# Sorting one 48-place block for two pairs of graphs at a time, and the last 16 places for four

## The chip, the cores and the metric

The kernel runs on one core of one Trainium2 chip. The metric is device time in microseconds (us), the median of three executions. A separate, profiled execution gives the page and the trace that this document reads. Its own time differs a little from the median, so shares and sums are made against the profiled execution.

## The reference

Sixteen graphs of 1,024 nodes with 64 channels pass through two layers. The first layer is the costly one. For each graph it takes a 0/1 adjacency, drops some edges of nodes with more than ten neighbours, and then, for each node and each channel by itself, sorts the values of the remaining neighbours and reads three quantiles:

```
nd = adj_d > 0
vals = jnp.where(nd[..., None], x[:, None, :, :], jnp.inf)
s = jnp.sort(vals, axis=2)
nv = nd.sum(2)
for tau, w in zip(TAUS, WTS):          # 0.25, 0.5, 0.75
    pos = tau * (nv - 1)               # v_lo, v_hi: s at floor(pos), ceil(pos)
    agg = agg + w * (v_lo + frac * (v_hi - v_lo))
h = relu((x + agg) @ W1 + b1);  y = (h @ W2 + b2) * mask
```

The second layer is three graph convolutions (adjacency times features times weights, with normalisation) and one product over their concatenation. Both layers start with a layer norm and end with a residual sum.

## The kernel before

**Pairs and places.** Graphs are worked in eight pairs (0 to 7): the 128 partitions are 2 graphs of 64 channels. For each graph, `prepare` ranks the nodes by their number of neighbours; the rank is the node's *place*. Places are cut into blocks of like degree, each with a number of slots that holds the neighbours of every node in it (`BLOCKS`, lines 39 and 40, as first place, end, fewest neighbours, slots):

```
BLOCKS = ((0, 200, 1, 11), (200, 392, 10, 13), (392, 592, 12, 15), (592, 768, 14, 17),
          (768, 888, 16, 19), (888, 960, 17, 21), (960, 1008, 19, 26))
TAIL = (1008, 1024, 21, 42)
```

Blocks are called 0 to 6 here; block 6 has 48 places, the tail 16.

**Gather and sort.** `gather` (line 959) brings the neighbours' values into slots: VectorE compares slot numbers (line 987) to make a one-hot tile `s`, TensorE multiplies it with the features `hp` into PSUM (line 1018), ScalarE copies the result to `g` (line 1023). `quantiles` (line 925) then runs a fixed comparator network of VectorE min and max instructions on `g` and a spare tile `t` (line 935; each instruction covers up to a two-dimensional grid of slots, times the width in places). ScalarE makes the coefficients from `z` (lines 868 and 871), and VectorE multiplies (941) and sums (950). The networks are tables in `NETS`, one for each number of slots: one row is one instruction. The number of elements that an instruction covers is its slots times the number of places sorted together.

**Order.** The program is emitted by generators. `weave` (line 1106) runs the sort of block n, and between its instructions takes steps of other generators by share of the sort's work: the gather of block n+1, and steps of `prepare` for the next pair (93 steps, split by `SHARES`; lines 31 and 1447). In the last sort (block 6), the next pair's block 0 is gathered. In pair 7, which has no next pair, seven steps of `later` (the rest of layer one, and layer two) stand beside each sort instead, and what is left of `later` follows the last sort. The framework's planner then orders each engine's instructions by the order of emission, by what is ready in its own model, and by which buffers are free. So an instruction can stand ahead of its place in the code.

**Preparation.** `prepare_one` loads the adjacency in eight rows of tiles `a`. ScalarE takes its sign (671), VectorE checks it for values other than 0 and 1 (673, into a throw-away tile `junk_v`), TensorE transposes (678). VectorE clears the diagonal by a multiplication with `other_h` (686). Then come the edge dropping (711 to 755), eight ScalarE passes that count larger keys (770, into `junk`), and GpSimd row writes of the edges to memory by place (`live_d`, 778). `find_live` loads them back by GpSimd (`lp`, 794, two buffers), transposes (809), counts, and `number_slots` (838) numbers the slots. The second half of the numbering falls into the next pair's first steps.

**Tails.** The tail of each of pairs 0 to 6 is gathered during the sort of block 5 of its own pair, stored (`tail_d`, line 1069), and sorted with others: pairs 0 to 3 in pair 4, pairs 4 to 6 in pair 7 (`TAILS`, line 43; `sort_tails`, line 1090). Pair 7's own tail is sorted alone at the end (line 1476, n = 7).

**Buffers.** `g` has two buffers, `t`, `z`, `coef` and `agg` one, `hp` two, `s` two, PSUM `pg` three.

## Time and profile before

| what | us |
| --- | --- |
| median of 3 executions | 3143.26 (3135.98 to 3146.2) |
| profiled execution, its own time | 3163.56 |
| its span, first to last instruction | 3161.8 |
| VectorE (DVE) busy | 2559.8 |
| TensorE (PE) busy | 2599.2 |
| ScalarE (ACT) busy | 1696.2 |
| GpSimd (POOL) busy | 619.5 |
| first sort instruction of pair 0, from the start | 230.3 |
| last sort instruction, from the start | 2832.2 |
| granted TensorE clock, mean | 0.915 of full |

The names in the page and the trace are PE for matmuls, PEld for weight loads, DVE for VectorE, ACT for ScalarE, POOL for GpSimd and SP for the queue of loads and stores. L935 is line 935 of the kernel before. A group's line has the tiles written and read, partitions by elements, the count, and after the bar the busy time. A stretch's line has its bounds and length, then each engine's busy time with its instructions, the granted clock, the share of the DMA engines and GB/s. A line of the timeline has the start, the time to the end of the last of its instructions, the engine and line, and in brackets the idle time before it and what ended it.

### The profile page before, as it was taken

The page shows a single profiled execution, that of the slowest core. Times are in us where ns is not written, and L with a number is a line of the kernel's source. Part 1 is how long each engine was busy: PE and PEld are TensorE (multiplying, and loading weights), DVE is VectorE, ACT ScalarE, POOL GpSimd, SP SyncE. Part 2 cuts the span into 40 slices and gives each one's busy share as a digit, 9 for nine tenths or more (in the row PEclk, how much of TensorE's full clock was granted, in tenths as well). Part 3 has the DMA queues.
Part 4 walks back from the last instruction along what each step waited for, and adds up shares of the span by engine and source line. Part 5 has one row for each costly group of instructions (what it writes and reads, how often), then busy time and mean ns, then how long its engine had stood idle before and what let it go on. Part 6 is the DMA issues. An engine that isn't in the chain of part 4 may idle for free.

```text
span 3161.8 us, 67201 instructions
## 1 busy us (share of the span) xinstructions
PE 2599.2 (82%) x27849; PEld 1697.4 (54%) x27849; DVE 2559.8 (81%) x5895; ACT 1696.2 (54%) x3292; POOL 619.5 (20%) x545
## 2 busy tenths in 40 slices
PE   2678978898888889885798889888986688977778
PEld 1445655565556556653565566456643456644445
DVE  4149889998999799989998999899976979963332
ACT  4764666567557755774367557745853223332221
POOL 5110161022102200330022103300422530311110
PEclk9779999999899999997899999999987799988989
DMA  4131022111211212122111211211113011122211
GB/s 138 46 104 60 3 67 70 56 55 52 66 57 54 64 56 68 46 72 47 42 64 51 66 56 57 67 56 63 48 36 75 9 41 26 49 55 54 54 54 42
DMA packets 221082, 177.45 MB, mean 56 GB/s; under 512 B 189024, under 2 KB 189152, under 8 KB 216672
## 3 DMA queue, kind: packets, MB, share of 16 engines
q1 hardware_dynamic: 141824, 125.88, 13.1%
q0 software_dynamic: 17408, 37.81, 3.9%
q10 hardware_dynamic: 61536, 9.39, 1.7%
q8 instruction: 219, 3.59, 0.5%
q14 instruction: 95, 0.78, 0.1%
HBM read 124.44 MB, written 48.55 MB: 55 GB/s over the span
## 4 chain that ended last, share of the span: by engine, by line
DVE 40%; PE 29%; ACT 12%; DMA 8%; issue 6%; another core or an unknown queue 2%; POOL 2%; ACTq 1%; DVEq 0%; POOLq 0%; SPq 0%
PE pg L1018 11%; DVE t L935 10%; DVE s L987 9%; DVE g L935 8%; PE pg L1200 5%; ACT junk L770 3%; DMA a<-in_adj 3%; DMA lp<-live_d 3%; DVE junk_v L673 2%; PE pr L845 2%; DVE g_tails L935 1%; DVE t_tails L935 1%; PE keys L763 1%; PE pf L1216 1%
## 5 line engine op out<-in xcount | busy, mean ns | idle before, releaser
L1018 PE MATMUL pg<-s,hp 128*64 128x400 bf16 (+11 forms) x16848 | 1366.5, 313 | 172.3 <-DVE s L987 138.1
L1018 PEld LDWEIGHTS <-hp 128*64 128x64 bf16 x16848 | 894.5, 112 | 553.9 <-issue 109.6
L987 DVE TENSOR_SCALAR s<-r 128x3200 bf16<-128x3200 bf16 (+25 forms) x1312 | 623.6, 521 | 103.6 <-PE pg L1018 74.9
L778 POOL DMA_INDIRECT live_d<-edge,place x128 | 261.1, 2040 | 1354.3 <-DVE place L773 1149.9
L1023 ACT COPY g<-pg 128x400 f32<-128x400 f32 (+10 forms) x384 | 169.0, 443 | 399.4 <-PE pg L1018 363.1
L935 DVE TENSOR_TENSOR t<-g 128x600 f32<-128x600 f32 (+9 forms) x524 | 315.5, 626 | 34.0 <-ACT g L1023 33.2
L1200 PE MATMUL pg<-adjT,xw 128*64 128x512 fp8e4 x2304 | 284.5, 398 | 52.8 <-ACT xw L1185 25.7
L935 DVE TENSOR_TENSOR g<-t 128x96 f32<-128x96 f32 (+16 forms) x555 | 283.2, 537 | 1.2
L1243 POOL DMA_INDIRECT agg<-agg_d,place x128 | 171.2, 1338 | 495.2 <-PE pt L1131 258.2
L671 ACT ACTIVATE edge<-a 128x1024 fp8e4<-128x1024 f32 x128 | 135.1, 1058 | 214.4 <-DMA a<-in_adj 213.9
L1200 PEld LDWEIGHTS <-xw 128*64 128x64 bf16 x2304 | 140.1, 114 | 182.4 <-issue 42.0
L868 ACT ACTIVATE coef<-z,bias 128x200 f32<-128x200 bf16 (+6 forms) x480 | 173.9, 405 | 102.3 <-DVE agg L950 66.0
L935 DVE TENSOR_TENSOR t<-t 128x192 f32<-128x192 f32 (+20 forms) x447 | 207.8, 475 | 0.2
L871 ACT ACTIVATE coef<-coef,wcol 128x200 f32<-128x200 f32 (+7 forms) x512 | 189.6, 403 | 9.3 <-issue 7.1
L673 DVE SCALAR_TENSOR_TENSOR junk_v<-a 128x1024 fp8e4<-128x1024 f32 x128 | 155.4, 1214 | 24.4 <-DMA a<-in_adj 24.4
L845 PE MATMUL pr<-liveT,upto 128*128 128x512 fp8e4 (+2 forms) x384 | 127.4, 350 | 53.1 <-ACT r L851 46.9
L770 ACT ACTIVATE junk<-keys,minus 128x1024 fp8e4<-128x1024 f32 x128 | 144.3, 1128 | 38.1 <-PE keys L763 34.3
L851 ACT CAST r<-pr 128x592 bf16<-128x592 f32 (+1 forms) x256 | 142.5, 585 | 41.1 <-PE pr L847 32.1
L794 POOL DMA_DIRECT2D lp<-live_d x128 | 89.4, 699 | 376.9 <-PE pt L809 319.3
L812 ACT ACTIVATE liveT<-pt 128x1024 fp8e4<-128x1024 f32 x128 | 130.3, 1034 | 50.5 <-PE pt L809 47.1
L752 ACT ACTIVATE edge<-q,bias 128x1024 fp8e4<-128x1024 f32 x128 | 141.8, 1108 | 22.6 <-PE q L747 22.6
L725 ACT ACTIVATE stays<-cs,back 128x1024 f16<-128x1024 f32 x128 | 136.7, 1111 | 31.1 <-PE cs L721 15.9
(182 smaller groups left out, 3879.4 us busy)
## 6 DMA issues: line engine op xcount, KB each, us to landing
a<-in_adj SPq DMA_DIRECT2D x128, 512.0 KB
adjT_d<-edgeT SPq DMA_DIRECT2D x16, 1024.0 KB
lp<-live_d POOLq DMA_DIRECT2D x128, 128.0 KB
adjT<-adjT_d SPq DMA_DIRECT2D x16, 1024.0 KB
room<-in_x SPq DMA_DIRECT2D x16, 256.0 KB
h_d<-room SPq DMA_DIRECT2D x16, 256.0 KB
h_again<-h_d SPq DMA_DIRECT2D x16, 256.0 KB
xt<-in_x SPq DMA_DIRECT2D x16, 256.0 KB
```

Of the source, the lines that this page charges most:

```text
L673: nc.vector.scalar_tensor_tensor(junk, a, 1.0, a, ALU.is_equal, ALU.not_equal, accum_out=odd[:, b, t : t + 1], saturate=False)
L770: nc.scalar.activation(junk, keys, AF.Sign, bias=minus[:, t : t + 1], accum_out=above[:, t : t + 1], saturate=False)
L778: sent = nc.gpsimd.indirect_dma_start(out=live_d[b][:, :], out_offset=bass.IndirectOffsetOnAxis(ap=place[:, b, t : t + 1], axis=0), in_=ed ...
L845: nc.tensor.matmul(out=pr[:, o], lhsT=upto, rhs=liveT[:, u, sl], start=True, stop=(u == 0))
L868: nc.scalar.activation(coef[:, i, :], z[:, at], AF.Abs, bias=bias(rank - (slots + 1) // 2 + tau), scale=sign)
L871: nc.scalar.activation(coef[:, i, :], coef[:, i, :], AF.Relu, bias=wcol[:, q : q + 1], scale=-w)
L935: nc.vector.tensor_tensor(view(bufs, o, n1, n2), view(bufs, a, n1, n2), view(bufs, b, n1, n2), ALU.max if op else ALU.min)
L987: nc.vector.tensor_scalar(s[:, k, :, us, w0:], r[:, :, us, at + w0 : at + W], float(LIVE + 1 + k0 + k), None, ALU.is_equal)
L1018: summed = nc.tensor.matmul(out=pg[x * C : (x + 1) * C, ks, w0:], lhsT=st.hp[:, part, x, u, :], rhs=s[:, ks, x, u, w0:], start=(whole and ...
L1023: nc.scalar.copy(g[:, k0 : k0 + n, :], pg)
L1200: nc.tensor.matmul(out=pg[cs, :], lhsT=part[:, u, cs], rhs=adjT[x][:, u, sl], start=(u == 0 and k == 0), stop=(u == NT - 1 and k == len(xw ...
L1243: nc.gpsimd.indirect_dma_start(out=agg[:, t, x, :], out_offset=None, in_=agg_d[b][:, :], in_offset=bass.IndirectOffsetOnAxis(ap=place[:, b ...
```

## The change

Block 6 (`MID`) is no longer sorted in each pair. An even pair gathers it during the sort of block 4, into the front of the buffer that block 5's gather fills next, and stores it in memory (`part_d`). The odd pair after it loads those rows into one half of a double-width tile, gathers its own block 6 into the other half, and sorts 96 places together (`rows_of_pairs`, `sort_pairs`). Even pairs so have six sorts, odd ones seven, and `SHARES` gets one row for each kind. In even pairs the next pair's block 0 and the tail are gathered during the sort of block 5.

The tails of pairs 4 to 7 are sorted together: pair 7's tail is gathered during its block 0, straight into the joint tile. Seven steps of `later` now stand beside that joint sort, and the separate last sort is gone.

Four networks are replaced. Instructions and comparator outputs (slots written) of each, before and after:

| slots | instructions | outputs | product instructions after it |
| --- | --- | --- | --- |
| 13 | 29, 29 | 85, 85 | 1, 1 |
| 15 | 31, 30 | 106, 106 | 1, 1 |
| 19 | 60, 57 | 158, 158 | 1, 2 |
| 26 | 95, 85 | 249, 249 | 1, 2 |

The network of 13 needs 15 spare slots instead of 17. The tail's (187 instructions, 550 outputs, 3 products) stays.

The diagonal is cleared by a bitwise and on 32-bit words. The two throw-away tiles share the two buffers of `lp`. In `later`, `h` lies in the buffer of the former `hp`. Aggregates of pairs 6 and 7 are complete only after the last joint sort (`done.sent`).

The diff, with the networks' rows and repeated edits left out:

```diff
-SHARES = (10, 9, 17, 24, 20, 13, 0)
+SHARES = ((12, 12, 21, 27, 21, 0), (10, 9, 17, 24, 20, 13, 0))
...
 
-TAILS = {4: (0, 4), 7: (4, 7)}
+TAILS = {4: (0, 4), 7: (4, 8)}
 TAIL = (1008, 1024, 21, 42)
+
...
-    13: (17, {3: 2, 4: 5, 5: 1, 6: 4, 7: 7, 8: 0, 9: 3, 10: 6}, (
...
+    13: (15, {3: 1007, 4: 1010, 5: 1006, 6: 1011, 7: 1009, 8: 1005, 9: 1012, 10: 1008}, (
...
-    15: (17, {3: 1001, 4: 1006, 5: 1003, 7: 1002, 8: 1000, 10: 1005, 11: 1004}, (
...
+    15: (17, {3: 7, 4: 4, 5: 9, 7: 8, 8: 6, 10: 5, 11: 10}, (
...
-    19: (24, {4: 8, 5: 5, 6: 6, 9: 4, 10: 9, 13: 10, 14: 7}, (
...
+    19: (24, {4: 1003, 5: 1016, 6: 1006, 9: 1012, 10: 1004, 13: 1014, 14: 1005}, (
...
-    26: (40, {6: 7, 7: 12, 8: 10, 9: 14, 12: 8, 13: 13, 17: 9, 18: 11, 19: 15}, (
...
+    26: (40, {6: 1000, 7: 1007, 8: 1002, 9: 1005, 12: 1003, 13: 1004, 17: 8, 18: 1001, 19: 1006}, (
...
+
+    off_diag = const.tile([P, P // 4], I32, name="off_diag")
+    nc.vector.tensor_scalar(off_diag[:, :].bitcast(U8), ident, -255.0, 255.0, ALU.mult, ALU.add)
...
-    TW = TAIL[1] - TAIL[0]
-    tail_d = [dram.tile([P, TAIL[3], TW], F32, name=f"tail_d{p}") for p in range(NP)]
-
-    tail_z = const.tile([P, len(TAUS), NP, TW], BF16, name="tail_z")
+    MW, TW = (b[1] - b[0] for b in (BLOCKS[MID], TAIL))
+    part_d = {
+        MID: [dram.tile([P, BLOCKS[MID][3], MW], F32, name=f"mid_d{p}") for p in range(NP)],
+        MID + 1: [dram.tile([P, TAIL[3], TW], F32, name=f"tail_d{p}") for p in range(NP)],
+    }
+
+    part_z = {
+        MID: const.tile([P, len(TAUS), 2, MW], BF16, name="mid_z"),
+        MID + 1: const.tile([P, len(TAUS), 4, TW], BF16, name="tail_z"),
+    }
...
     def diagonal(e):
 
+        e = e[:, :, :].bitcast(I32)
         dims = [list(d) for d in e.ap]
-        return bass.AP(tensor=e.tensor, offset=e.offset, ap=[dims[0], [N + P, NT], [1, P]])
+        return bass.AP(tensor=e.tensor, offset=e.offset, ap=[dims[0], [(N + P) // 4, NT], [1, P // 4]])
 
...
             nc.scalar.activation(edge[:, t, :], a, AF.Sign, saturate=False)
-            junk = work.tile([P, N], F8, tag="junk_v", name="junk_v")
+            junk = work.tile([P, N // 4], I32, tag="lp", bufs=2, name="junk_v")[:, :].bitcast(F8)
...
         own = diagonal(edgeT)
-        nc.vector.tensor_tensor(own, own, other_h[:, None, :].to_broadcast([P, NT, P]), ALU.mult, saturate=False)
+        nc.vector.tensor_tensor(own, own, off_diag[:, None, :].to_broadcast([P, NT, P // 4]), ALU.bitwise_and)
...
         for t in range(NT):
-            junk = work.tile([P, N], F8, tag="junk", name="junk")
+            junk = work.tile([P, N // 4], I32, tag="lp", bufs=2, name="junk")[:, :].bitcast(F8)
             nc.scalar.activation(
...
 
-    def gather_block(st, n, pools, home=None):
+    def gather_block(st, n, pools, home=None, into=None, first=-0.2, end=0.9):
+
 
         work, ps, rows = pools
         block = (BLOCKS + (TAIL,))[n]
@@ -1060,20 +1066,24 @@
         pool, tag, bufs = home or (rows, "g", 2)
 
         def groups():
-            if n == 0:
+            if n >= MID:
+                z = part_z[n]
                 for q in range(len(TAUS)):
-                    nc.gpsimd.tensor_copy(tail_z[:, q, st.p, :], st.z[:, q, TAIL[0] : TAIL[1]])
-            st.g[n] = pool.tile([P, slots, j1 - j0], F32, tag=tag, bufs=bufs, name="g")
-            send(pools, (yield from gather(st, block, st.g[n], pools)))
-            if n == len(BLOCKS) and st.p < NP - 1:
-                nc.scalar.dma_start(out=tail_d[st.p][:, :, :], in_=st.g[n])
-
-        return Steps(groups()), -(-slots // per_group(block)), -0.2, 0.9
+                    nc.gpsimd.tensor_copy(z[:, q, st.p % z.shape[2], :], st.z[:, q, j0:j1])
+            to = into
+            if to is None:
+                to = st.g[n] = pool.tile([P, slots, j1 - j0], F32, tag=tag, bufs=bufs, name="g")
+            send(pools, (yield from gather(st, block, to, pools)))
+            in_place = st.p % 2 if n == MID else st.p == NP - 1
+            if n >= MID and not in_place:
+                nc.scalar.dma_start(out=part_d[n][st.p][:, :, :], in_=to)
+
+        return Steps(groups()), -(-slots // per_group(block)), first, end
 
     def sort_block(st, n, pools):
 
         work, ps, rows = pools
-        block = (BLOCKS + (TAIL,))[n]
+        block = BLOCKS[n]
         j0, j1, _, slots = block
         if n == 0:
 
@@ -1082,26 +1092,32 @@
             st.done = 0
         t = rows.tile([P, plan(block)[3], j1 - j0], F32, tag="t", bufs=1, name="t")
         yield from quantiles(work, block, (st.g[n], t), st.z[:, :, j0:j1], st.agg[:, j0:j1])
-        while st.done + P <= j1 or (j1 >= TAIL[0] and st.done < j1):
+        while st.done + P <= j1 or (n == MID - 1 and st.done < j1):
             cols = slice(st.done, min(st.done + P, j1))
             waiting.append((st.p, st.agg, cols, st.done))
             st.done = cols.stop
 
-    def sort_tails(first, end, pools):
+    def rows_of_pairs(n, first, end, sent, pools):
 
         work, ps, rows = pools
-        W = (end - first) * TW
-        g = rows.tile([P, TAIL[3], W], F32, tag="g", bufs=2, name="g_tails")
+        block = (BLOCKS + (TAIL,))[n]
+        W = block[1] - block[0]
+        g = rows.tile([P, block[3], (end - first) * W], F32, tag="g", bufs=2, name="g_pairs")
+        for p in range(first, sent):
+            nc.scalar.dma_start(out=g[:, :, (p - first) * W : (p - first + 1) * W], in_=part_d[n][p][:, :, :])
+        return g
+
+    def sort_pairs(n, first, end, g, pools):
+
+        work, ps, rows = pools
+        block = (BLOCKS + (TAIL,))[n]
+        W = block[1] - block[0]
+        whole = (end - first) * W
+        t = rows.tile([P, plan(block)[3], whole], F32, tag="t", bufs=1, name="t_pairs")
+        agg = work.tile([P, whole], F32, tag="agg_pairs", name="agg_pairs")
+        yield from quantiles(work, block, (g, t), part_z[n].rearrange("p q p2 w -> p q (p2 w)"), agg)
         for p in range(first, end):
-            nc.scalar.dma_start(out=g[:, :, (p - first) * TW : (p - first + 1) * TW], in_=tail_d[p][:, :, :])
-        yield 0.0
-        t = rows.tile([P, plan(TAIL)[3], W], F32, tag="t", bufs=1, name="t_tails")
-        agg = work.tile([P, W], F32, tag="agg_tails", name="agg_tails")
-        yield from quantiles(
-            work, TAIL, (g, t), tail_z[:, :, first:end].rearrange("p q p2 w -> p q (p2 w)"), agg
-        )
-        for p in range(first, end):
-            waiting.append((p, agg, slice((p - first) * TW, (p - first + 1) * TW), TAIL[0]))
+            waiting.append((p, agg, slice((p - first) * W, (p - first + 1) * W), block[0]))
 
     def weave(sort, *others):
 
...
             nc.sync.dma_start(out=rows_of(graphs[x]), in_=res[:, :, x, :])
         yield
 
-    def later(pools, done):
+    def later(pools, keep, done):
 
         one, ps = pools
+
+        old_hp = keep.tile([P, 3, 2, NT, C], BF16, tag="hp", bufs=2, name="old_hp")
 
         def first(p):
             assert p < done.sent
             xt = one.tile([P, NT, 2, C], F32, tag="xt", bufs=2, name="xt")
-            h, agg = (one.tile([P, NT, 2, C], F32, tag=k, name=k) for k in ("h", "agg"))
+            h = old_hp.rearrange("p a x t c -> p (a x t c)")[:, : 2 * N * 2 * C // P].bitcast(F32)
+            h = h.rearrange("p (t x c) -> p t x c", x=2, c=C)
+            agg = one.tile([P, NT, 2, C], F32, tag="agg", name="agg")
             mk = one.tile([P, NT, 2], U8, tag="mk", name="mk")
             mask = one.tile([P, NT, 2], F32, tag="mask", name="mask")
...
@@ -1443,25 +1462,39 @@
                     return (yield from prepare(p + 1, early))
 
                 ahead = Steps(coming(st, p))
-                for n in range(last):
-                    steps = (ahead, SHARES[n], 0.0, 1.0)
+
+                paired = p % 2
+                for n in range(MID + paired):
+                    steps = (ahead, SHARES[paired][n], 0.0, 1.0)
+                    sort = sort_block(st, n, pools) if n < MID else sort_pairs(MID, p - 1, p + 1, both, pools)
                     if n == 0 and p in TAILS:
 
-                        tails = sort_tails(*TAILS[p], pools)
-                        next(tails)
-                        weave(sort_block(st, n, pools), steps)
-                        weave(tails, gather_block(st, n + 1, pools))
-                    elif n == last - 1:
+                        tails = rows_of_pairs(MID + 1, *TAILS[p], TAILS[p][1], pools)
+                        weave(sort, steps)
+                        weave(sort_pairs(MID + 1, *TAILS[p], tails, pools), gather_block(st, n + 1, pools))
+                    elif n == MID - 1 + paired:
                         ahead.rest()
                         to_come = ahead.result
-                        weave(sort_block(st, n, pools), gather_block(to_come, 0, pools))
-                    elif n == last - 2:
+                        tail = () if paired else (gather_block(st, MID + 1, pools, (early[0], "a", 2)),)
+                        weave(sort, *tail, gather_block(to_come, 0, pools))
+                    elif n == MID - 1:
+                        both = rows_of_pairs(MID, p - 1, p + 1, p, pools)
                         weave(
-                            sort_block(st, n, pools), gather_block(st, n + 1, pools),
-                            gather_block(st, last, pools, (early[0], "a", 2)), steps,
+                            sort, gather_block(st, MID, pools, into=both[:, :, MW:]),
+                            gather_block(st, MID + 1, pools, (early[0], "a", 2)), steps,
+                        )
+                    elif n == MID - 2 and not paired:
+
+                        j0, j1, _, slots = BLOCKS[n + 1]
+                        room = st.g[n + 1] = pools[2].tile([P, slots, j1 - j0], F32, tag="g", bufs=2, name="g")
+                        size = BLOCKS[MID][3] * MW
+                        mid = room.rearrange("p s w -> p (s w)")[:, :size].rearrange("p (s w) -> p s w", w=MW)
+                        weave(
+                            sort, gather_block(st, MID, pools, into=mid, end=0.35),
+                            gather_block(st, n + 1, pools, into=room, first=0.4), steps,
                         )
                     else:
-                        weave(sort_block(st, n, pools), gather_block(st, n + 1, pools), steps)
+                        weave(sort, gather_block(st, n + 1, pools), steps)
                 st = to_come
             for _ in st.number:
                 pass
@@ -1472,20 +1505,23 @@
             late = (one, inner.enter_context(tc.tile_pool(name="ps_late", bufs=2, space=PSUM)))
             done = Pair()
             done.sent = TAILS[NP - 1][0]
-            ahead = Steps(later(late, done))
-            for n in range(last + 1):
+            ahead = Steps(later(late, keep, done))
+            for n in range(MID):
                 steps = (ahead, STEPS, 0.0, 1.0)
+                sort = sort_block(st, n, pools)
                 if n == 0:
-                    tails = sort_tails(*TAILS[NP - 1], pools)
-                    next(tails)
-                    weave(sort_block(st, n, pools), steps)
-                    weave(tails, gather_block(st, n + 1, pools))
+                    tails = rows_of_pairs(MID + 1, *TAILS[NP - 1], NP - 1, pools)
+                    weave(sort, gather_block(st, MID + 1, pools, into=tails[:, :, -TW:]), steps)
+                    weave(sort_pairs(MID + 1, *TAILS[NP - 1], tails, pools), gather_block(st, n + 1, pools), steps)
                     continue
-                if n < last:
-                    weave(sort_block(st, n, pools), gather_block(st, n + 1, pools), steps)
+                if n < MID - 1:
+                    weave(sort, gather_block(st, n + 1, pools), steps)
                 else:
-                    weave(sort_block(st, n, pools), steps)
-                done.sent = NP - 1
+                    both = rows_of_pairs(MID, NP - 2, NP, NP - 1, pools)
+                    weave(sort, gather_block(st, MID, pools, into=both[:, :, MW:]), steps)
+
+                done.sent = NP - 2
+            weave(sort_pairs(MID, NP - 2, NP, both, pools), (ahead, STEPS, 0.0, 1.0))
             send(pools)
             done.sent = NP
             ahead.rest()
```

## The prediction

> **What bounds the kernel now.** I read the page first (engine shares, the forty slices, the chain), then cut the span into stretches, then looked at single instructions inside them. From the page, the busy times, the slices and the chain's shares by engine:
>
> ```profile
> PE 2599.2 (82%) x27849; PEld 1697.4 (54%) x27849; DVE 2559.8 (81%) x5895; ACT 1696.2 (54%) x3292; POOL 619.5 (20%) x545
> ...
> PE   2678978898888889885798889888986688977778
> DVE  4149889998999799989998999899976979963332
> ...
> DVE 40%; PE 29%; ACT 12%; DMA 8%; issue 6%; another core or an unknown queue 2%; POOL 2%; ACTq 1%; DVEq 0%; POOLq 0%; SPq 0%
> ```
>
> VectorE is at nine tenths from slice 3 to slice 35 and TensorE close behind; only the first three slices and the last four (the second half of the network, 330 us) are not VectorE's. Averages hide which of the two ends last, so I took the starts of each block's first sort instruction as cuts. A "stretch" is the time from one block's first sort instruction to the next one's. The seven stretches (blocks 0 to 6) of pair 5, columns length, then busy PE, PEld, DVE, ACT, POOL with their instructions, clock, DMA:
>
> ```profile
> 1789.90:1825.30 35.40, 32.70 (x397) 21.75 (x393) 34.58 (x48) 19.93 (x42) 0.00 (x0) 0.95 0.15 48
> 1825.30:1865.30 40.00, 33.48 (x429) 23.11 (x427) 40.00 (x58) 17.91 (x35) 0.00 (x0) 1.00 0.23 82
> 1865.30:1914.00 48.70, 45.68 (x563) 31.60 (x560) 48.70 (x81) 29.94 (x50) 0.00 (x0) 1.00 0.14 45
> 1914.00:1960.20 46.20, 40.85 (x486) 29.16 (x486) 44.92 (x88) 34.28 (x63) 23.36 (x10) 0.93 0.15 51
> 1960.20:2003.50 43.30, 38.75 (x449) 25.87 (x447) 40.20 (x122) 35.08 (x66) 13.60 (x13) 0.98 0.19 53
> 2003.50:2041.10 37.60, 34.08 (x392) 19.64 (x392) 29.59 (x102) 29.77 (x66) 9.68 (x11) 0.98 0.23 67
> 2041.10:2083.80 42.70, 34.70 (x345) 19.52 (x346) 42.12 (x127) 24.18 (x54) 8.67 (x3) 0.88 0.25 77
> ```
>
> Six of seven are VectorE's to within 3 us. Only stretch 5 (block of 72 places) leaves it idle, 8 us: there the preparation of the next pair binds. The sum is 293.9 us, DVE 280.1, PE 260.2. So VectorE work taken out of a stretch should come off the time, until PE or the preparation binds.
>
> In pair 7 (no next pair; steps of the second half are woven in), the tails' sort, block 6 and the lone tail of 16 places:
>
> ```profile
> 2440.30:2491.60 51.30, 19.17 (x187) 14.24 (x185) 51.30 (x209) 13.23 (x46) 37.64 (x15) 0.68 0.09 21
> ...
> 2747.00:2782.80 35.80, 32.94 (x293) 21.04 (x294) 34.84 (x136) 13.90 (x34) 3.38 (x4) 0.95 0.11 19
> 2782.80:2832.20 49.40, 36.20 (x258) 21.76 (x254) 33.06 (x210) 15.71 (x49) 12.36 (x13) 0.83 0.27 75
> ```
>
> **What an instruction costs.** The timeline of VectorE inside the lone tail:
>
> ```profile
> 2807.43 0.17 DVE L935 TENSOR_TENSOR t<-g,t 128x16 f32<-128x16 f32 x1
> 2807.51 0.21 DVE L935 TENSOR_TENSOR g<-g 128x64 f32<-128x64 f32 x1
> 2807.65 0.16 DVE L935 TENSOR_TENSOR g<-g,t 128x16 f32<-128x16 f32 x1
> 2807.73 0.18 DVE L935 TENSOR_TENSOR g<-t 128x32 f32<-128x32 f32 x1
> ```
>
> Durations overlap: 0.17 us is printed, but the next starts 0.08 us later. What counts is start to start: 0.14 us for 64 elements, 0.08 to 0.09 for 16, that is about 0.069 us plus 1/0.96 ns an element, and the same line fits wider instructions (0.90 us for 800). The whole lone tail checks it: 194 instructions, 9,296 elements: 13.4 + 9.7 = 23.1 us; lines 935, 941 and 950 took 22.66 + 0.64 + 1.33 = 24.6. A removed instruction is thus worth 0.07 us, not its printed 0.16 to 0.2.
>
> **What the skill says.** The Trainium skill, "VectorE: DVE Perf Modes", section on the TRN2 errata, gives 58 cycles plus one per element for such an operation (60 ns fixed; the trace has 69), and its tier table holds f32 tensor_tensor to one element a cycle; the trace agrees. The same section says to reinterpret narrow data as INT32 to cut the element count; no run here shows that yet. "Perfetto Trace Analysis", Identifying the Most-Contended Engine, says [...]weight-load busy is the better gauge: here 89% against 58% in pair 5, so I take PE to have room. Stretch 2 backs it: DVE at 100% with PEld at 65%.
>
> **The change, part by part.**
>
> *Block 6.* Lines 935, 941, 950 in stretch 6 took 19.76 + 0.60 + 0.94 = 21.3 us (100 instructions, 12,768 elements: by the formula 6.9 + 13.3 = 20.2). For two pairs: 91 instructions (85 network, 2 products, 4 sums), twice the elements: 6.3 + 26.6 = 32.9, scaled by 21.3/20.2: 34.6. An even pair (0, 2, 4, 6) loses 21.3, an odd one gains 13.3.
>
> *Diagonal.* From the tile view of line 686:
>
> ```profile
> L686 DVE TENSOR_TENSOR edgeT<-edgeT,other_h x16: 1204/1217/1260, 60.1 to 2240.6; 128x1024 fp8e4<-128x1024 fp8e4 x16
> ```
>
> 1,024 elements become 256: 768/0.96 = 0.80 us each if the bitwise operation also runs at one element a cycle. Bounds: 0 (four cycles an element) to 0.80; I take 0.80, two a pair: 1.6.
>
> *Other networks.* Blocks of 15 and 19 slots lose 1 and 2 instructions: 0.2 us a pair. That of 13 keeps 29.
>
> So even pairs −23.1, odd pairs +13.3 − 1.8 = +11.5; pairs 0 to 6: 4 × (−23.1) + 3 × 11.5 = −57.9. The two diagonals before pair 0: −1.6.
>
> *Pair 7.* The lone stretch goes (−49.4). Its tail enters the joint sort of four: 16 more places × 581 / 0.96 = 9.7 by the formula; but the four-pair sort of pair 4 took 50.2 against 42.6 here, so +7.6. Its seven steps move into that sort, now 51.3 us long with PE at 19.2: their VectorE part, 33.1 − 24.6 = 8.4, plus waits. Stretch 1 of pair 7, with seven steps in it, is 54.1 us long at 45.1 of DVE, so 9 are waits; I take 6. Block 6: +13.3. Nets −0.2. Sum −14.3.
>
> *Moved and hidden.* Even pairs do 93 preparation steps in five stretches instead of six, with block 6's gather in stretch 4 and the tail's in stretch 5. That work (PE about 21 us of steps from stretch 5, 12 of gather) goes under stretches 0 to 4, 215 us long at PEld 65% or less: nothing. If that cover is gone, it is rival A. Block 6's rows leave for memory from the buffer that block 5's gather then fills: 128 rows of 5 KB; the store of a 1 MB tile took 3.9 us on the chain, and the gap between the two gathers is 0.19 of a 50 us stretch, some 10 us: nothing; 4 × 4 = 16 us if uncovered. They come back as 3,328 pieces of 192 bytes, issued on ACT's queue one stretch (38 us) ahead. Pair 4's 21,504 pieces of 64 bytes took about 16 us, so about 2.5 us each time: hidden. Issuing a tail took 0.6 us of ACT (3.9 at most), ACT at 54%. Sixteen more agg stores and POOL's copies of z: off the path. The network of 26 is wider, so t grows; h lives in the old hp: same waits as before.
>
> *The added wait.* junk_v (DVE), junk (ACT) and lp (POOL's loads) now share two buffers. POOL's timeline in pair 3:
>
> ```profile
> 1314.49 1.46 POOL L794 DMA_DIRECT2D lp<-live_d  x2 [2.00 <-DMA live_d<-edge,place]
> 1334.38 0.54 POOL L794 DMA_DIRECT2D lp<-live_d  x1 [18.43 <-PE pt L809]
> 1338.62 1.85 POOL L794 DMA_DIRECT2D lp<-live_d  x1 [3.71 <-PE pt L809]
> ```
>
> Two loads of the first graph hold both buffers from 1314 until the transposes (line 809) read them at 1333 and 1338, and line 770's eight passes for the second graph ran on ACT from 1332.7 to 1346. With a shared pair these passes wait for the transposes and the loads for the passes. Queued behind on ACT are copies of g (line 1023) that free PSUM for the gathers; behind POOL's loads are the second graph's row writes (line 778), and the preparation chain that binds stretch 5 waits for those. A load that can't run ahead costs its issue, 0.5, and landing, 2.4 us (chain): up to 8 × 2.9 = 23 us a pair; at least 0 (sharing adds waits only). I take 2.5 a pair, seven pairs: +17.5, since passes and loads overlap for only half of the eight.
>
> **Sum.** −57.9 − 1.6 − 14.3 + 17.5 = −56.3 on the profiled execution's 3163.6 us (span 3161.8): 3107. The runs' median, 3143.3, lies 20 us lower, so 3087, −1.8%.
>
> **Rivals.**
>
> A: TensorE binds in even pairs. For: PE busy 260 in 294. If 0.94 (stretch 2) is the ceiling, an even pair can't go under 260/0.94 = 277: it gains 17, not 23, and the sum is −32: 3111. Against: weight loads at 58%.
>
> B: more is won. Stretch 5's idle 8 us goes in even pairs, whose preparation is done earlier: 4 × 8 more: 3055.
>
> C, the other side: the shared buffers. At 5.5 of the eight loads exposed, 16 us a pair, 112 in all against 74 won: +38, 3181. It decides from (73.8 + 9.4)/7 = 11.9 us a pair. For: the two uses do overlap in the trace; SP's loads, the row writes and the gathers sit behind. Against: most stretches are VectorE's, and the preparation has slack in all but stretch 5.
>
> D: the diagonal's 32-bit form runs at a quarter of the rate: 13 us lost, 3100; still faster.
>
> **How the numbers follow.** Forecast with D 0.46 (own range 3060 to 3112), A 0.15, B 0.10, C 0.22, half of C's price, landing level, 0.07. A measurement here tells about 0.3%, 9.4 us. Faster 0.46 + 0.15 + 0.10 = 0.71, same 0.07, slower 0.22. The range runs from 3040 (B with some spare) to 3180 (C at its price), leaving out 0.05 below and 0.12 above.
>
> **What would show it.** Right: even pairs near 273 us, odd near 307; block 6's sort about 35 us every second pair; line 686's successor near 0.4 us; some 58 us less DVE busy in pairs 0 to 6. Wrong: ACT's line 770 waiting for line 809, or POOL's lp loads for ACT (C); even pairs at 280 or more with DVE idle before the gather's compares, waiting for PE (A). The sum would fail if a reordered plan opened idle time on VectorE in stretches that have none now.

## The result and the profile after

The changed kernel takes 3312.9 us (median of four runs, 3311.4 to 3316.5); the kernel before took 3144.7 (3136.0 to 3150.1) on the same chip. The ratio is 1.0539, 95% interval 1.0514 to 1.0565: 168 us slower, where 1.8% faster was forecast, and above the forecast's 3040 to 3180. The profiled execution's span is 3311.5 us against 3161.8.

The page of the changed kernel: engine shares, the slices of TensorE and VectorE, and the chain's shares by engine.

```profile
PE 2599.0 (78%) x27857; PEld 1717.4 (52%) x27857; DVE 2508.7 (76%) x5242; ACT 1685.0 (51%) x3196; POOL 552.5 (17%) x569
...
PE   3468889986888788867587998688886679878878
DVE  3228879976999698969987897699967788984332
...
PE 3%; DVE 1%; ACT 0%; issue 0%; POOL 0%; DMA 0%; POOLq 0%; DVEq 0%
```

VectorE's busy time fell by 51 us (2559.8 to 2508.7) with 653 instructions fewer, so the work that was to go has gone. The time went into idleness: VectorE's slices, mostly eights and nines before, now have more holes of 6 and 7. The chain of waits breaks off after 4% of the span and says nothing here, so the stretches must. Those of pair 5, blocks 0 to 6 in order (length, busy PE, PEld, DVE, ACT, POOL, clock, DMA share, GB/s):

```profile
1892.30:1925.10 32.80, 30.68 (x370) 19.83 (x368) 32.80 (x45) 18.67 (x43) 0.00 (x0) 1.00 0.12 37
1925.10:1963.10 38.00, 34.16 (x421) 23.36 (x419) 37.90 (x55) 18.51 (x35) 0.00 (x0) 0.96 0.20 65
1963.10:2004.40 41.30, 40.25 (x480) 27.53 (x479) 41.09 (x64) 22.96 (x39) 0.00 (x0) 1.00 0.02 8
2004.40:2078.10 73.70, 57.91 (x636) 41.01 (x633) 56.39 (x112) 50.30 (x85) 9.73 (x8) 0.88 0.24 75
2078.10:2114.90 36.80, 24.60 (x331) 18.01 (x329) 36.66 (x114) 21.61 (x49) 15.60 (x3) 0.89 0.10 23
2114.90:2178.30 63.40, 44.23 (x471) 25.90 (x472) 34.51 (x107) 37.94 (x74) 19.61 (x23) 0.80 0.27 72
2178.30:2230.00 51.70, 41.63 (x430) 25.02 (x431) 51.37 (x115) 31.07 (x64) 9.54 (x6) 0.93 0.22 64
```

Stretch 6 is the block of 48 places for two pairs, 51.7 us long with VectorE busy for 51.4 of it. The damage is in stretch 3 (73.7 us against 46.2) and stretch 5 (63.4 against 37.6, VectorE idle for 29). In stretch 2 there is less of everything than before (41.3 against 48.7): work of the preparation has moved out of it into stretch 3.

Lines of the changed kernel's preparation and gather lie five further on than before: 678 is the check of the adjacency, 775 the key passes, 783 the row writes, 799 their loads, 814 the transposes of what was loaded, 992 the gather's compares and 1023 its matmuls. What moved shows in two views by line in pair 1, from 680 to 702 us: line 775 (ACT) and line 678 (VectorE), with count, least/median/most ns, first and last start. The two graphs in them are those of pair 2, which is being prepared.

```profile
L775 ACT ACTIVATE junk<-keys,minus x8: 1105/1121/1144, 687.9 to 695.5; 128x1024 fp8e4<-128x1024 f32 x8
```

```profile
L678 DVE SCALAR_TENSOR_TENSOR junk_v<-a x3: 1221/1222/1227, 695.7 to 701.1; 128x1024 fp8e4<-128x1024 f32 x3
```

The three checks belong to the second graph. The first of them begins at 695.7 us, when the first graph's last key pass but one, started at 694.5, has ended. In the kernel before, the same step in pair 3 ran at 1243.6 to 1266, ahead of the first graph's passes (1274.7 to 1286). The intake of the second graph, with the two adjacency buffers that it holds, has been put behind the first graph's keys. Then GpSimd's timeline in pair 1 (start, length, what it waited for in brackets):

```profile
707.97 1.62 POOL L783 DMA_INDIRECT live_d<-edge,place  x1 [0.30 <-issue]
765.46 0.58 POOL L799 DMA_DIRECT2D lp<-live_d  x1 [55.87 <-DVE s L992]
766.56 0.57 POOL L799 DMA_DIRECT2D lp<-live_d  x1 [0.52 <-ACT junk L775]
767.44 18.78 POOL L783 DMA_INDIRECT live_d<-edge,place  x1 [0.30 <-issue]
...
794.14 0.96 POOL L783 DMA_INDIRECT live_d<-edge,place  x1 [0.30 <-issue]
795.10 1.15 POOL L799 DMA_DIRECT2D lp<-live_d  x2
```

The first graph's rows are written by 710 us, but its first load comes at 765, just after the second graph's last key pass (763.9 to 765). The view puts the first load's wait down to a compare of VectorE and the second's to the key passes; a wait for several things is named after one of them. Over the whole changed kernel loads waited for the key passes eleven times (total us, times, longest), and in the kernel before never:

```profile
POOL lp L799 <- ACT junk L775: 155.3, 11, 51.4
```

The first graph's third load stands behind the second graph's eight row writes and comes at 795. Who pays, from the waits of 765 to 848 us, in the same form:

```profile
PEld L814 <- DMA lp<-live_d: 34.9, 12, 24.4
ACT liveT L817 <- PE pt L814: 32.0, 6, 25.0
DVE s L992 <- PE pg L1023: 29.0, 3, 26.3
```

TensorE stands at line 814 with a load that comes 24 us late, the gather's matmuls stand behind it, and VectorE's compares behind these: stretch 5.

### The profile page after: what moved, and what is told of

Its sections match the earlier page's. It is cut to its first block, busy times and chain, and to the rows that moved or that the text cites. A ratio compares the mean times of both kernels' runs of the same rounds, so it can differ in the third digit from the quotient of the medians.

```text
span 3311.5 us, 66628 instructions
## 1 busy us (share of the span) xinstructions
PE 2599.0 (78%) x27857; PEld 1717.4 (52%) x27857; DVE 2508.7 (76%) x5242; ACT 1685.0 (51%) x3196; POOL 552.5 (17%) x569
## 5 line engine op out<-in xcount | busy, mean ns | idle before, releaser
L783 POOL DMA_INDIRECT live_d<-edge,place x128 | 213.7, 1670 | 1200.7 <-DVE place L778 996.1
L1028 ACT COPY g<-pg 128x400 f32<-128x400 f32 (+8 forms) x366 | 160.2, 445 | 397.0 <-PE pg L1023 388.6
L940 DVE TENSOR_TENSOR t<-g 128x800 f32<-128x800 f32 (+20 forms) x416 | 299.7, 746 | 5.4 <-ACT g L1028 4.2
L940 DVE TENSOR_TENSOR g<-t 128x800 f32<-128x800 f32 (+5 forms) x392 | 268.5, 716 | 1.4
L814 PE MATMUL pt<-ident_h,lp 128*128 128x128 bf16 x1024 | 93.3, 250 | 177.8 <-DMA lp<-live_d 176.4
L683 PE MATMUL ptE<-ident_h,edge 128*128 128x128 bf16 x1024 | 91.5, 243 | 140.4 <-ACT edge L676 112.5
L873 ACT ACTIVATE coef<-z,bias 128x200 f32<-128x200 bf16 (+4 forms) x392 | 150.5, 423 | 94.3 <-DVE agg L955 60.3
L814 PEld LDWEIGHTS <-lp 128*128 128x128 fp8e4 x1024 | 72.1, 112 | 207.3 <-DMA lp<-live_d 200.9
L876 ACT ACTIVATE coef<-coef,wcol 128x200 f32<-128x200 f32 (+6 forms) x460 | 173.6, 413 | 0.8 <-issue 0.5
L940 DVE TENSOR_TENSOR t<-t 128x600 f32<-128x600 f32 (+18 forms) x272 | 172.4, 644 | 0.7
```

What stands on the lines that cost most here:

```text
L783: sent = nc.gpsimd.indirect_dma_start(out=live_d[b][:, :], out_offset=bass.IndirectOffsetOnAxis(ap=place[:, b, t : t + 1], axis=0), in_=ed ...
L814: nc.tensor.matmul(out=pt[:, u, :], lhsT=lp[:, u * P : (u + 1) * P], rhs=ident_h, start=True, stop=True)
L873: nc.scalar.activation(coef[:, i, :], z[:, at], AF.Abs, bias=bias(rank - (slots + 1) // 2 + tau), scale=sign)
L876: nc.scalar.activation(coef[:, i, :], coef[:, i, :], AF.Relu, bias=wcol[:, q : q + 1], scale=-w)
L940: nc.vector.tensor_tensor(view(bufs, o, n1, n2), view(bufs, a, n1, n2), view(bufs, b, n1, n2), ALU.max if op else ALU.min)
L1028: nc.scalar.copy(g[:, k0 : k0 + n, :], pg)
```

## The experiments

Ratios are to runs of the kernel before on the same chip, taken in turn; one part in 300 is about what can be told apart. "Keys" below is the throw-away tile of the key passes and of the last check, "intake" that of the adjacency's check.

**1. All tiles apart.** Everything of the change, but intake has its own buffer, the eight key passes write to eight places of `stays`, which is done with by then, the last check works in place, and a constant of 512 bytes is let go after its use.

```diff
-junk = work.tile([P, N // 4], I32, tag="lp", bufs=2, name="junk_v")[:, :].bitcast(F8)
+junk = work.tile([P, N], F8, tag="junk_v", name="junk_v")
-junk = work.tile([P, N // 4], I32, tag="lp", bufs=2, name="junk")[:, :].bitcast(F8)
+junk = stays[:, t, : N // 2].bitcast(F8)
```

> The changed kernel with the throw-away tiles taken out of lp's two buffers: junk_v has a buffer of its own again, the key-counting passes write into the graph's finished edge tile, and the last check writes in place. All other parts of the change stay. Theory S (the shared pair of buffers costs the time: a tile of that tag cannot be had before the one two places ahead in the emitted order is free, so the second graph's intake waits for the first graph's key passes and lp's loads for the second graph's): about 3070, the 74 us that the prediction's sum has without the sharing; 3040 to 3110. Theory R (the regrouping costs it: even pairs squeeze 93 steps into five stretches, TensorE or the preparation binds in stretches 3 to 5): 3270 to 3313, as the changed kernel.

3169.5 us, ratio 1.0069 (1.0042 to 1.0097). Sharing the buffers is most of the loss, but neither theory's range holds: the other half of theory S, a kernel clearly faster than before, didn't come either.

**2 to 4. The sharing alone, in the kernel before**: all three uses in lp's two buffers (second), keys with lp (third), keys with intake in two buffers of their own (fourth). The line below is of the second and third; the second does the same to intake, and the fourth gives both the tag `junk` with two buffers.

```diff
-junk = work.tile([P, N], F8, tag="junk", name="junk")
+junk = work.tile([P, N // 4], I32, tag="lp", bufs=2, name="junk")[:, :].bitcast(F8)
```

> The kernel before with nothing changed but the tags: junk_v and junk go into lp's two buffers. Theory S: 150 to 240 us slower than before, 3290 to 3385, with the start of pair 0's sort some 21 us later as in the changed kernel, and stretches 3 and 5 long. Theory R: 3140 to 3165.

> The kernel before with only junk (ScalarE's key passes) in lp's two buffers; junk_v keeps its own. Splits theory S: if lp's loads standing behind the second graph's key passes (and then behind GpSimd's row writes) are the larger part, 3230 to 3320; if the second graph's intake standing behind the first graph's passes is, 3143 to 3190. Theory R: 3140 to 3160.

> The kernel before with junk_v and junk in two buffers of their own, lp's kept apart. Splits theory S the other way: if the second graph's intake standing behind the first graph's key passes is the larger part, 3230 to 3320; otherwise 3143 to 3190. Theory R: 3140 to 3160.

Ratios 1.0817 (1.0779 to 1.0854), 1.0292 (1.0242 to 1.0342) and 1.0557 (1.0511 to 1.0603): +251, +88 and +172 us, and 88 + 172 is 260. The first is above theory S's 150 to 240; of the two pairings, keys with intake is the larger, but the other is far from nothing. They hurt in different places. Stretches 3 and 5 of pair 1, for all three together, keys with lp, and keys with intake:

```profile
714.40:782.60 68.20, 52.85 (x627) 37.81 (x624) 56.52 (x110) 46.82 (x78) 10.08 (x8) 0.92 0.25 81
820.00:883.30 63.30, 43.60 (x465) 26.56 (x469) 30.72 (x104) 37.65 (x74) 17.94 (x22) 0.79 0.21 62
```

```profile
703.80:751.20 47.40, 39.11 (x485) 27.55 (x486) 46.64 (x93) 35.31 (x65) 9.01 (x8) 0.96 0.14 50
790.20:840.10 49.90, 43.07 (x464) 25.75 (x468) 31.01 (x105) 37.41 (x73) 8.04 (x15) 0.89 0.20 58
```

```profile
703.30:770.40 67.10, 52.07 (x626) 36.97 (x623) 56.42 (x109) 46.77 (x78) 11.22 (x10) 0.92 0.27 86
817.10:858.40 41.30, 36.86 (x424) 21.45 (x424) 30.60 (x103) 33.73 (x71) 4.48 (x9) 0.99 0.19 53
```

Keys with intake stretches stretch 3 (45.8 before) to 67, keys with lp stretches stretch 5 (42.9 before) to 50, and all three together give both. Pair 1 is a mild case of keys with lp: its stretch 4 is 6 us shorter (39.1), and the whole pair only 0.8 longer. Pairs 0 and 5 are 23 and 19 longer, 21 and 23 of it in stretch 5.

**5. Eight places or one.** As the first, but all key passes write to one place.

```diff
-junk = stays[:, t, : N // 2].bitcast(F8)
+junk = stays[:, 0, : N // 2].bitcast(F8)
```

> The changed kernel with the throw-away tiles apart again, but with all eight key passes of a graph writing the same kilobyte (stays[:, 0]), one after the other, as in the kernel before; in the last run they wrote eight different places, and ACT's order had all eight in a row, GpSimd's row writes came 9 us earlier and stood ahead of the other graph's lp loads. Theory O (that order cost the last run its start and part of the even pairs): first sort at 229 to 232 us instead of 241, lp loads no longer waiting up to 35 us, time 3115 to 3145 where the kernel before takes 3151. Theory Q (the even pairs are squeezed whatever the order, and pair 7 gained nothing): only the start comes back, 3155 to 3165.

Ratio 0.9979 (0.9962 to 0.9996). The first sort starts at 228.7 us instead of 240.9. On this chip the kernel before took 3169.6 us, so theory O's 3115 to 3145 where that takes 3151 is a ratio of 0.989 to 0.998: it holds, at its upper end, and is right about the start. Its other part, that even pairs gain, isn't shown: they take 1209.4 us in the profiled executions of both runs, on chips where the kernel before takes 3151.2 and 3169.6. With eight places ACT ran all passes in a row, those of the first graph from 92.3 to 101 us; with one, each depends on the one before it, and the planned order put copies of the other graph between them (92.4 to 108) and the row writes later. The first experiment thus had a flaw of its own: taking a dependency away moved work as well.

**6. Without regrouping.** The kernel before with the diagonal's bitwise and and the new networks only.

```diff
-nc.vector.tensor_tensor(own, own, other_h[:, None, :].to_broadcast([P, NT, P]), ALU.mult, saturate=False)
+nc.vector.tensor_tensor(own, own, off_diag[:, None, :].to_broadcast([P, NT, P // 4]), ALU.bitwise_and)
```

> The kernel before with the diagonal as a bitwise and on 256 words and with the new networks, nothing grouped and no tile shared. By the sum of the prediction: two diagonals of 0.8 us and 0.2 us of networks a pair, 1.6 ahead of pair 0, and nine instructions of 0.07 us fewer in each of eight block-6 sorts: 14.2 + 5 = 19 us less (ratio 0.994). Rival: part of it falls into stretches where the preparation binds: 5 to 10 us less (0.997 to 0.998). Second rival: the order written by the planner moves and hides all of it: within 3 us.

Ratio 1.0007 (0.9994 to 1.0021): the second rival. VectorE's busy time did fall by 18 us:

```profile
PE 2566.1 (81%) x27826; PEld 1694.8 (54%) x27849; DVE 2541.9 (80%) x5800; ACT 1699.2 (54%) x3292; POOL 639.5 (20%) x545
```

In pairs 1 to 6 stretch 2 was 3 to 5 us shorter and stretch 6 was 4 to 7 us longer, with work moved into the last: TensorE is busy for 40.3 us in stretch 6 of pair 5, where it was 34.7. That the moved order, rather than another bound, took up the gain is argued from this, not shown.

**7. Pair 7 as before.** The fifth ("the first run" in the two texts on record that follow), with the last pair's tail sorted alone at the end and no steps in the joint tail sort.

```diff
-weave(sort_pairs(MID + 1, *TAILS[NP - 1], tails, pools), gather_block(st, n + 1, pools), steps)
+weave(sort_pairs(MID + 1, *TAILS[NP - 1], tails, pools), gather_block(st, n + 1, pools))
...
+weave(sort_pairs(MID + 1, NP - 1, NP, last_tail, pools), (ahead, STEPS, 0.0, 1.0))
```

> As the first run of this call, but pair 7's tail as in the kernel before: the tails of pairs 4 to 6 together without steps of the second half in that sort, and pair 7's own 16 places last, with seven steps in them. The prediction took 27 us for joining them (49.4 less 7.6, 8.4 and 6). If that was right, this is 27 us slower than the first run. Theory L (in pair 7 the steps of the second half bind, and a load of the aggregates that lay under the stepless sort is now waited for: 65 us of such waits against 23): within 6 us of it. If joining did harm: 10 us or more faster.

Ratio 0.9991 (0.9976 to 1.0006) beside the fifth's 0.9979: 4 us apart by these ratios, with intervals that overlap. Pair 7 takes 479.8 us in this one's profile and 473.2 in the fifth's. The 27 us that joining the tails was to bring aren't there; theory L.

**8. Steps earlier in even pairs.**

```diff
-SHARES = ((12, 12, 21, 27, 21, 0), (10, 9, 17, 24, 20, 13, 0))
+SHARES = ((16, 15, 23, 23, 16, 0), (10, 9, 17, 24, 20, 13, 0))
```

> As the first run of this call, but an even pair's 93 preparation steps are 16, 15, 23, 23, 16 over its five stretches instead of 12, 12, 21, 27, 21. Theory D (the steps are only badly spread: 27 in stretch 3 and 21 in stretch 4 are more than these hide): even pairs fall by 8 to 14 us each, 30 to 50 us in all. Theory A (the preparation as a whole, PE and the chain of its waits, sets the length of an even pair, wherever the steps are): even pairs keep their length within 4 us, and the time is within 12 us of the first run.

Ratio 1.0005 (0.999 to 1.002). Against the fifth's profile even pairs fell by 0.8 to 3.2 us each; odd pairs rose by 0.4, 10.8 and 4.5. Theory A.

**9 and 10. The one pairing left, and the cure.** The kernel before with only intake in lp's buffers; then the changed kernel with only keys taken out of them (512 bytes from a constant that is let go after its use).

```diff
-junk = work.tile([P, N // 4], I32, tag="lp", bufs=2, name="junk")[:, :].bitcast(F8)
+junk = work.tile([P, N], F8, tag="junk", name="junk")
```

> The kernel before with only the intake's throw-away tile (junk_v) in lp's two buffers, the key passes' one left alone: the one pairing of the three not yet run. Theory T (buffers of one tag are given out in the order in which the program asks for them, and what hurts is a wait against the order of the work: graph 2's intake behind graph 1's key passes, graph 1's loads behind graph 2's key passes): the order asked is all intakes of a pair, then its loads, so nobody waits against the order of work: 0 to 10 us more (ratio 1.000 to 1.003). Against the additive sum: 251 for all three together less 88 and less 171 is -8, the same. Rival (any throw-away tile in lp's buffers costs, since lp holds both for 20 us at a time): 60 to 90 us more, 1.02 to 1.03.

> The changed kernel with one line undone: the key passes (and the last check) write to a tile of their own, while the intake's throw-away tile stays in lp's buffers; the room comes from the 512 bytes of a constant that is kept no longer than it is used. Theory T: nearly all of the loss goes, the ratio is that of the kernel with all tiles apart, 0.995 to 1.001. Rival: the third pairing costs here too: 1.02 or more.

Ratios 1.0008 (0.9985 to 1.003) and 0.9966 (0.9949 to 0.9984), theory T in both. Intake in lp's buffers costs nothing that can be told; keys in them cost the changed kernel everything. GpSimd in pair 1 of the tenth:

```profile
693.54 0.96 POOL L783 DMA_INDIRECT live_d<-edge,place  x1 [0.30 <-DMA live_d<-edge,place]
696.51 1.52 POOL L799 DMA_DIRECT2D lp<-live_d  x2 [2.00 <-PE q L752]
...
721.48 0.54 POOL L799 DMA_DIRECT2D lp<-live_d  x1 [2.58 <-PE pt L814]
```

The first load follows the row writes by 2 us, not 56, and six loads are out before the second graph's rows (from 724). Where the keys write was worth 5.7% (1.0539 over 0.9966).

**11. Aggregates a pair ahead.** The tenth with two buffers for the second half's gathered aggregates (room from one buffer for `rest` and `res`).

```diff
-agg = one.tile([P, NT, 2, C], F32, tag="agg", name="agg")
+agg = one.tile([P, NT, 2, C], F32, tag="agg", bufs=2, name="agg")
```

> As the run before it, with two buffers for the gathered aggregates of the second half (rest and res of the second half share one buffer to make room), so that a pair's 16 gathers need not wait until the pair ahead has left the buffer. Theory L (in pair 7 the chain of the second half's steps sets the length, and in it the 20 to 25 us of gathers that VectorE's sum then waits for, 41 to 65 us in pair 7): 30 to 60 us less than the run before it, most of it in pair 7. Rival (the steps' other links, matmuls and their copies, take up the room): within 10 us.

3124.8 us (median of four runs, 3119.6 to 3150.5), ratio 0.9865 (0.9804 to 0.9926), 1.35% better than the kernel before: the fastest here. Pair 7 as a whole in the tenth and in this one:

```profile
2348.60:2830.00 481.40, 379.43 (x3399) 260.32 (x3399) 375.45 (x824) 139.44 (x336) 91.35 (x80) 0.84 0.18 42
```

```profile
2362.90:2813.90 451.00, 366.37 (x3403) 247.30 (x3399) 374.98 (x824) 139.19 (x336) 157.54 (x96) 0.88 0.21 46
```

VectorE is busy for 375 us in both, and pair 7 is 30 us shorter; what follows it fell from 331 to 312. VectorE's waits for the aggregates in pair 7, in the same order:

```profile
DVE agg L1158 <- DMA agg<-agg_d,place: 37.9, 3, 13.9
```

```profile
DVE agg L1158 <- DMA agg<-agg_d,place: 9.3, 1, 9.3
```

Theory L: with no less VectorE work, pair 7 shrinks when a link of the second half's chain goes.

**12. Less sorting in even pairs.** The tenth, with the sorts of blocks 3 and 4 of pairs 0, 2, 4 and 6 doing only half of their columns (that half of the work is left out).

```diff
+cut = 2 if n in (3, 4) and st.p % 2 == 0 else 1
-dims.append(list(last))
+dims.append([last[0], last[1] // cut])
```

> The kernel with the key passes apart, of two calls ago in its form without the second buffer for the aggregates, with part of the work left out: in pairs 0, 2, 4 and 6 the sorts of blocks 3 and 4 do only the first half of their columns (as many instructions, half the elements), so that VectorE has 20 to 24 us less to do in stretches 3 and 4 of an even pair. Nothing else is changed. Theory V (the prediction's: in an even pair VectorE's work is what ends last): each of the four even pairs falls by 20 us, 80 in all, ratio 0.971. Theory A (TensorE and the preparation's chain end last there, in stretch 3 with PE at 53.5 of 55.4 us): each falls by less than 6 us, 0 to 24 in all, ratio 0.989 to 0.998.

Ratio 1.0006 (0.9987 to 1.0024). Stretches 3 and 4 of pair 2 in the tenth, then in this one:

```profile
953.50:1008.90 55.40, 53.47 (x670) 37.65 (x670) 49.35 (x100) 43.80 (x82) 14.18 (x12) 1.00 0.19 59
1008.90:1076.90 68.00, 55.15 (x611) 32.31 (x613) 52.47 (x140) 50.05 (x95) 18.61 (x26) 0.90 0.26 75
...
sum 282.60, PE 251.87 PEld 169.36 DVE 259.62 ACT 181.97 POOL 32.78; mean PE 41.98 PEld 28.23 DVE 43.27 ACT 30.33 POOL 5.46
```

```profile
960.30:1019.30 59.00, 54.90 (x661) 37.06 (x657) 37.34 (x99) 46.59 (x90) 11.68 (x12) 0.97 0.20 59
1019.30:1078.80 59.50, 54.27 (x595) 31.12 (x599) 37.98 (x135) 45.67 (x86) 20.17 (x27) 0.94 0.21 66
...
sum 280.00, PE 257.61 PEld 172.81 DVE 234.72 ACT 176.62 POOL 31.85; mean PE 42.93 PEld 28.80 DVE 39.12 ACT 29.44 POOL 5.31
```

VectorE has 25 us less to do and the pair is 2.6 us shorter. The four even pairs together lose 97 us of VectorE's busy time (1083.7 to 986.3) and 7.6 us of length: theory A's length, and not theory V's 80. VectorE's sorting isn't what ends them. The time as a whole is still above theory A's range, since the three odd pairs, from which nothing was taken, grew by 21 us (924.9 to 946.0); why they did wasn't tried. The planned order moved in this run too: stretch 0 of pair 2 has 372 matmuls instead of 332. TensorE is busy for 91 to 97% of these stretches except stretch 4 of the tenth (81%); how much is its rate and how much the preparation's chain isn't separated.

## Why the prediction was wrong

The span's parts in the profiled executions, us: before, changed with the keys apart (the tenth), and as changed. The forecast column is the prediction's own sum without its shared-buffer term. (Runs in turn put the tenth 0.34%, 11 us, under the kernel before; single executions differ by as much. On the tenth's chip the kernel before takes 3169.0.)

| part | before | keys apart | difference | forecast | as changed | shared keys |
|---|---|---|---|---|---|---|
| to the first sort | 230.3 | 228.7 | -1.6 | -1.6 | 251.2 | +22.5 |
| pairs 0, 2, 4, 6 | 1263.3 | 1195.0 | -68.3 | -92.4 | 1251.0 | +56.0 |
| pairs 1, 3, 5 | 885.5 | 924.9 | +39.4 | +34.5 | 1014.7 | +89.8 |
| pair 7 | 453.2 | 481.4 | +28.2 | -14.3 | 476.3 | -5.1 |
| the rest | 329.5 | 331.0 | +1.5 | 0 | 318.3 | -12.7 |
| sum | 3161.8 | 3161.0 | -0.8 | -73.8 | 3311.5 | +150.5 |

**The step that failed first is "The added wait"**, "I take 2.5 a pair" with bounds 0 to 23. In pairs 0 to 6 the sharing cost 146/7 = 21 us a pair (14 in an even pair, 30 in an odd one), close to the bound and past the 11.9 from which rival C decides; and the start, with no sort to hide it, lost another 22.5, which no term held. Three things were wrong in it.

Its own reason doesn't give its number. "Only half of the eight" loads at 2.9 us is 11.6 a pair, 81 in all, against the 73.8 won: level, not faster. The 2.5 is less than one load.

It looked at one meeting of the three uses, passes against loads, and priced a late load by its own issue and landing, 2.9 us. The load isn't just late by itself: it waits until the other graph's passes are through (GpSimd idle for 55.9 us in the trace), and the third then stands behind eight row writes on GpSimd's queue. The text named those writes and didn't price them. And the larger loss, 172 us against 88 in the kernel before, is the pairing that it named (junk_v with junk) and didn't price: an intake of VectorE that waits for ACT's passes of the graph before, holding the adjacency's two buffers meanwhile. Rival C, at 0.22, had the right culprit and the right sign, by the same one meeting and the same price for a load; the measured 3312.9 is 132 us above its 3181.

What decides between harmless and harmful, as the changed kernel and runs 2, 3, 4, 9 and 10 show, is the order in which the program asks for the tiles: intake 1, keys 1, intake 2, keys 2, loads 1, loads 2 (with a last check, which also writes to keys, after each graph's loads). Two buffers in turn tie each use to the one two requests earlier, as the check that began at 695.7 us was tied to the last pass but one. Intake and loads lie in the order in which the work flows anyway (ratio 1.0008); keys 1 before intake 2, and keys 2 before loads 1, turn "later in the program" into "must wait", where the work had run the other way round. The trace of the kernel before had both facts: line 673 of the second graph ahead of line 770 of the first, and loads of the first graph ahead of the second's passes. The prediction read only the second. The Trainium skill, "Perfetto Trace Analysis", Optimization Strategy, says that a gap which repeats on the engine that should be full can mean too few buffers; VectorE's 29 us in stretch 5 of pairs 1 and 5 are such a gap.

**Even pairs: -17.1 each, not -23.1.** The step was "That work ... goes under stretches 0 to 4 ... PEld 65% or less: nothing". Block 6's stretch left, but what it had covered went into two others: in pair 2 stretch 3 grew from 48.0 to 55.4 us and stretch 4 from 47.7 to 68.0, for the 42.9 that went. This is rival A's size, and pairs 2 and 6 (282.6 and 277.0) stand at its 277 or above, not at 273. Run 8 speaks against the spread of the steps and run 12 against VectorE as the reason; whether TensorE itself, as rival A has it, or the chain of the preparation sets the length is open. The prediction had read TensorE's busy share of 89% in pair 5 as leaving room, since weight loads were busy for 58%. The reason given against A, low weight-load share, came from the Trainium skill, "Perfetto Trace Analysis", Identifying the Most-Contended Engine. Here stretch 3 of pair 2 has matmuls busy for 53.5 of 55.4 us at weight loads of 37.7 (68%), and halving the sort lengthened it to 59.0: a low share of weight loads did not mean that there was room.

**Pair 7: +28.2, not -14.3.** The step was "So VectorE work taken out of a stretch should come off the time", applied where the second half's chain sets the pace. Block 6's +13.3 and the tail's -27 were both in VectorE's coin; in the tenth the joint tail sort's stretch was 38 us longer than the tail sort's before (forecast 22), the last sort's 28 longer than block 6's (forecast 13.3) and the other stretches 11 longer, for the 49.4 that went. Joining brought nothing measurable (run 7), and one link of the chain was worth 30 us (run 11). VectorE waited for aggregates for 22.6 us in pair 7 of the kernel before, and for 60.1 in run 7, which has the same tails. Why the changed kernel has more of these waits stays open; that h now lives in the old hp wasn't tried apart.

**What held.** Block 6 for two pairs: lines 940, 946 and 955 in stretch 6 of pair 5 (tenth) took 31.9 + 1.1 + 1.4 = 34.4 us, forecast 34.6. Odd pairs: +39.4 for +34.5. The start: -1.6. The diagonal, in the tile view of the changed kernel:

```profile
L691 DVE TENSOR_TENSOR edgeT<-edgeT,off_diag x16: 418/426/439, 58.6 to 2377.5; 128x256 int32<-128x256 int32 x16
```

1217 to 426 ns, 0.79 us saved for 0.80 forecast, which settles rival D: 768 elements fewer saved 1.03 ns each, so the 32-bit form isn't slower by the element. VectorE's busy time in pairs 0 to 6 of the changed kernel fell by 49 us (2004.8 to 1955.4), forecast 58. So the durations were right or nearly so; it was their worth that wasn't. Run 6 is the plainest case: 18 us of VectorE saved, nothing gained.

## What to carry to other kernels

Before two tiles share a tag, write down the order in which the program asks for them beside the order in which they are used in the trace: here sharing was free where both agreed, and where they crossed it tied one piece of work to another, with all that is queued behind the late one as its price. A busy share of 95% doesn't make an engine the one that ends last: take work away from it in one stretch and look whether the stretch shrinks, before a plan rests on it. And when an experiment takes a dependency away, look what else moved; a tile written only to be thrown away was also what kept eight passes apart.

## What the hardware showed unexpectedly

One row write in some pairs holds GpSimd far longer than the rest: 18.8 us at 767 us in the changed kernel and 20.2 at 664 in the tenth, where most take about 1; in the kernel before eight of 128 took 11.9 to 19.9 us. It isn't always the second graph's. What holds it wasn't tried, but the traces give a lead. All 14 writes of over 5 us in these three kernels lie where VectorE runs two-input instructions and compares without a break, and each ends 0.8 to 1.0 us, the length of a short write, after VectorE's first pause (10 of them) or its first small copy from PSUM (4). Many short writes lie in such stretches too, so this alone isn't the cause. In the first run none of the 128 took over 5 us. In the changed kernel loads stood behind it: it is 18.8 of the 28.5 us between the second and the third load.
